# Queries and keys of an attention kernel by seven half products in place of eight

## The chip, the cores and the metric

One core of a Trainium2 chip runs the whole program; the time is device microseconds of that core. The engines that matter are PE (TensorE, matrix products into PSUM), DVE (VectorE), ACT (ScalarE), POOL (GpSimd, which works on SBUF only), and SP, whose queue issues nearly all DMAs. Each engine takes its instructions in order and waits for the others by semaphores. The order on every engine is written out by hand in this kernel.

## The reference, cut to what matters

Two attention layers run one after the other over 4 images of 32x32 tokens with 768 channels, 12 heads of 64. Each layer normalizes by groups of channels, projects to queries, keys and values, adds relative-position terms to the scores, and projects the result back. Everything is float32.

```python
def _L0_conv_ref(x, Wqkv, Wproj, bproj, rel_pos_h, rel_pos_w):
    ...
    qkv = x @ Wqkv
    ...
    q, k, v = (qkv[0], qkv[1], qkv[2])
    ...
    scores = scale * jnp.einsum('bqc,bkc->bqk', q, k) + bias
    attn = jax.nn.softmax(scores, axis=-1)
    out = jnp.einsum('bqk,bkc->bqc', attn, v)
    ...
    return out @ Wproj + bproj
...
x = x + _L0_conv_ref(_gn(x), ...)
x = x + _L1_conv_ref(_gn(x), ...)
```

Layer 1 is of the same form, with biases on queries, keys and values.

## The kernel before

The kernel walks over 8 images (4 for each layer) and, in each, over 6 pairs of heads; `g` counts the 48 pairs. A pair is 8 units, one for each 128 query tokens (`n` = 0 to 7). A unit emits, in this order: the DMAs in the list `early`; `biases` for the unit two ahead (two POOL additions of 128x1024, L323); `scores` for the unit one ahead (PE L337, then on DVE an addition with a minimum, L346, then the exponential on ACT, L350); the reads of turned weights that have come due; up to 3 steps of `take` (in unit 7 alone); `turn` for the present unit (two DVE transposes L370, then a DMA to memory, read back later as `pt`); `divide` for the unit one ahead (reciprocal on DVE L358, then head 0 is scaled on POOL L362 and head 1 on ACT L364); the rest of `take`; and in units 2 and 6 `weigh` (PE L399, the weighted sum of values, copied out by ACT as `attn`).

`take` hands out the steps of the list `todo`: the projections that the next pair needs (`prepare`) and a share of the output projection (`put_out`, in unit 7). `shares` says how many steps each unit takes. A projection of queries or keys, `project_in`, makes 512 tokens of one of the two: 6 chunks of 128 channels, and for each chunk two products of 64 rows, one in the upper half and one in the lower half of the array's rows (L215). The two halves go to two banks of PSUM; ACT copies one out and DVE adds the other (L228/L230, L231). A pair has four such groups, eight half products over the 64-row halves of the channels. `project_values` makes 256 tokens of values for two pairs at once, in the same two row halves (L250, evacuated by L260 on ACT and L261 on DVE, two of each in alternation). `positions` (PE L282, ACT L287 and L297) and `diagonals` (8 small DMAs, L309) make the position terms from 512 tokens of queries.

All PE results but the scores share one ring of two PSUM tiles, `ps_m`: a group of matmuls starts when the group two before it in the order of PE has been evacuated. The scores have a ring of their own, `ps_s`. Six `sc` tiles hold the scores of three units.

Near the end of an image the next one is prepared: its normalization statistics are gathered in pair 3 (`norm`), and in pair 4 `apply` normalizes its six tiles of 128x1024 in place on DVE (L194): one in each of units 2, 4 and 6, and three in unit 7.

Of the kernel before, what the change touches and what calls it, by code (L numbers as in the profile page):

```python
# [36 lines left out]
P = 128  # L37
# [13 lines left out]
AHEAD = 3  # L51
# [3 lines left out]
def attention_blocks(ctx: ExitStack, tc: tile.TileContext, a: dict, out: bass.AP):  # L55
# [4 lines left out]
    wpool = ctx.enter_context(tc.tile_pool(name="weights", bufs=2))  # L60
    wopool = ctx.enter_context(tc.tile_pool(name="wo", bufs=2))
    xpool = ctx.enter_context(tc.tile_pool(name="x", bufs=NC + AHEAD))
    apool = ctx.enter_context(tc.tile_pool(name="attn", bufs=6))
    qkpool = ctx.enter_context(tc.tile_pool(name="qk", bufs=2))
    vpool = ctx.enter_context(tc.tile_pool(name="v", bufs=3))
    scpool = ctx.enter_context(tc.tile_pool(name="sc", bufs=6))
    tmppool = ctx.enter_context(tc.tile_pool(name="tmp", bufs=2))
    tbpool = ctx.enter_context(tc.tile_pool(name="tb", bufs=2))
    ptpool = ctx.enter_context(tc.tile_pool(name="pt", bufs=2))
    relpool = ctx.enter_context(tc.tile_pool(name="rel", bufs=2))  # L70
    iopool = ctx.enter_context(tc.tile_pool(name="io", bufs=4))
# [15 lines left out]
    xn_of, w_of, wo_of = {im: [] for im in range(NI)}, {}, {}  # L87

    def load_x(im, c, chunk=None):

        l, b = images[im]
        if c == len(xn_of[im]):
            xn_of[im].append(xpool.tile([P, S], FP, tag="xn", name=f"xn_{im}_{c}"))
        chunk = c if chunk is None else chunk
        nc.sync.dma_start(out=xn_of[im][c], in_=srcs[l][b][chunk * P : (chunk + 1) * P, :])

    def load_w(g, which):

        im, pair = divmod(g, NP)
        if which == 2:  # L100
            w = wpool.tile([P, NC, 2 * P], FP, tag="wv", bufs=1, name=f"wv_{g}")
            src = a[f"wv{images[im][0]}"][pair // 2]
        else:
            w = wpool.tile([P, NC, P], FP, tag="w", name=f"w_{g}_{which}")
            src = a[f"wqk{images[im][0]}"][pair, which]
        w_of[g, which] = w
        nc.sync.dma_start(out=w, in_=src.rearrange("p (c o) -> p c o", c=NC))

    for c in range(NC):
        load_x(0, c)  # L110
    for which in range(3):
        load_w(0, which)
# [35 lines left out]
    def stats(im, c, i, x):  # L148

        if i == 0:  # L150
            half_stats[im] = small.tile([P, 2, 6], FP, tag="st", name=f"st_{im}_{c}")
        st = half_stats[im]
        nc.vector.bn_stats(st[:, i, :], x)  # L153
        if i == 1:
            nc.vector.bn_aggr(mv_of[im][:, c, :], st.rearrange("p i s -> p (i s)"))

    def norm(im):
# [13 lines left out]
        def gather():  # L171
            queue.dma_start(out=per.rearrange("(c p) s -> p c s", p=P), in_=mv_of[im])
# [11 lines left out]
        def inverses():  # L184
            nc.vector.reciprocal(mv[:, 2, 0:1], mv[:, 2, 1:2])
            for k, x in enumerate((mv[:, 0, 0:1], mv[:, 2, 0:1])):
                nc.vector.tensor_copy(g[:, 1, :, k], x.to_broadcast([NG, GS]))
            queue.dma_start(out=back.rearrange("(g k) s -> g k s", k=GS), in_=g[:, 1, :, :])

        def spread():  # L190
            queue.dma_start(out=nrm, in_=back.rearrange("(c p) s -> p c s", p=P))

        def apply(c):
            nc.vector.tensor_scalar(  # L194
                xn_of[im][c], xn_of[im][c], nrm[:, c, 0:1], nrm[:, c, 1:2], ALU.subtract, ALU.mult
            )

        return {1: gather, 2: by_group, 4: groups, 5: inverses, 7: spread}, apply


    qk_of, v_of, rel_of, t_of = {}, {}, {}, {}

    def project_in(g, which, i):

        im, pair = divmod(g, NP)
        xn, w = xn_of[im], w_of[g, which]
        cols = slice(i * HALF, (i + 1) * HALF)
        if i == 0:
            tag = "qk"[which]
            qk_of[g, which] = qkpool.tile([P, S], FP, tag=tag, name=f"{tag}_{g}")  # L210
        t = ps_m.tile([P, 2, HALF], FP, tag="m", name=f"pj_{g}_{which}_{i}")
        for c in range(NC):
            for a in range(2):
                rows = slice(a * D, (a + 1) * D)
                nc.tensor.matmul(  # L215
                    t[:, a, :], lhsT=w[rows, c, :], rhs=xn[c][rows, cols],
                    start=(c == 0), stop=(c == NC - 1),
                )
            if c < NC - 1:
                yield True  # L220
        to, t = qk_of[g, which], [t[:, a, :] for a in range(2)]
        if which == 1:
            to = to.rearrange("p (a m) -> p a m", a=4)[:, :, i * P : (i + 1) * P]
            t = [x.rearrange("p (m a) -> p a m", a=4) for x in t]
        else:
            to = to[:, cols]
        if images[im][0] == 0:
            nc.scalar.copy(to, t[0])  # L228
        else:
            nc.scalar.activation(to, t[0], AF.Identity, bias=bqkv[:, which, pair : pair + 1])  # L230
        nc.vector.tensor_tensor(to, t[1], to, ALU.add)  # L231
        if which == 0:
            (later if g else mid).append(lambda: positions(g, i))
        if i == 1 and g + 1 < NPAIR:
            later.append(lambda: load_w(g + 1, which))
        yield True

    def project_values(g, i):

        im, pair = divmod(g, NP)  # L240
        xn, w = xn_of[im], w_of[g, 2]
# [4 lines left out]
        for k in range(2):  # L246
            for c in range(NC):
                for a in range(2):
# [3 lines left out]
                        lhsT=xn[c][rows, (2 * i + k) * P : (2 * i + k + 1) * P], rhs=w[rows, c, :],  # L252
# [9 lines left out]
        if i == 3:  # L262
            if g + 2 < NPAIR:
# [422 lines left out]
```

## Time and profile before

| | before |
|---|---|
| median of 3 runs | 3512.72 us (3509.97 to 3515.46) |
| the profiled execution | 3513.09 us, of which the span is 3511.3 us |
| granted TensorE clock | 0.998 |
| busy: DVE, ACT, POOL | 2306.5, 1810.3, 2290.3 us |
| DMA | 1046.75 MB, mean 298 GB/s |
| steady period of one pair (start of an output projection to the next, 317.60 to 389.29) | 71.69 us |
| the same where an image ends (389.29 to 462.05) | 72.76 us |

A busy share is the time in which an engine has an instruction in work. The chain of waits is the work that ended last, followed back from the end of the program; a stretch that is wholly on PE in it is one in which PE waited for nothing. In the timeline each line has the start, the length, the engine, the line of the kernel, the operation, what it writes and reads, and in brackets how long the engine was idle before it and what it waited for. Lengths of successive DVE instructions overlap a little: an addition of 692 ns on 512 elements is followed by the next instruction 0.61 us after its start, a pair of transposes takes 2.28 us, and two L346 take 2.29 us.

### The profile page before, as it was taken

The numbers are of one execution on the slowest core, as the hardware profiler recorded it, in microseconds if no ns is written. First come the engines' busy times: TensorE is split into PE (matmuls) and PEld (weight loads), VectorE is DVE, ScalarE is ACT, GpSimd is POOL, SyncE is SP. The second block draws the span as 40 slices with busy tenths as digits, with TensorE's granted clock in tenths as the row PEclk, the third lists the DMA queues.
The fourth block names the chain that finished last, engine by engine and source line by source line (L and its number), as shares of the span: only waits on it lengthen the run. The fifth ranks groups of instructions, "written<-read, shape, count | busy, mean of one in ns | idle before, by whom it ended". The sixth has DMA issues, their size and how long they took to land.

```text
span 3511.3 us, 55069 instructions
## 1 busy us (share of the span) xinstructions
PE 3460.9 (99%) x21120; PEld 1920.0 (55%) x21120; DVE 2306.5 (66%) x3532; ACT 1810.3 (52%) x2913; POOL 2290.3 (65%) x1154
## 2 busy tenths in 40 slices
PE   6999999999999999999999999999999999999998
PEld 3555555555555555555555555555555555555553
DVE  4766767767677676666766667666666666666665
ACT  3555545554545545455545555455545555455543
POOL 3776666666666666666666666666666666666662
PEclk9999999999999999999999999999999999999999
DMA  3988988889898888988888988888888888888877
GB/s 129 321 299 290 322 306 308 316 285 316 301 321 308 295 313 290 320 303 285 310 306 314 305 287 309 311 305 300 297 305 316 307 292 301 310 297 291 293 275 264
DMA packets 520407, 1046.75 MB, mean 298 GB/s; under 512 B 142672, under 2 KB 205648, under 8 KB 470992
## 3 DMA queue, kind: packets, MB, share of 16 engines
q1 hardware_dynamic: 465648, 1015.81, 82.9%
q10 hardware_dynamic: 54496, 27.43, 2.6%
q8 instruction: 166, 2.72, 0.3%
q14 instruction: 97, 0.79, 0.1%
HBM read 568.01 MB, written 475.10 MB: 297 GB/s over the span
## 4 chain that ended last, share of the span: by engine, by line
PE 94%; DVE 2%; DMA 2%; issue 1%; ACT 0%; SPq 0%; DVEq 0%; ACTq 0%
PE pj L215 26%; PE av L399 19%; PE s L337 19%; PE pv L250 14%; PE o L471 14%; PE tp L282 2%; DMA td<-tb 1%; DVE tb L370 1%; DVE sc L346 1%; DMA pt<-td 0%; DVE st L153 0%; DVE q L231 0%; DVE res L482 0%; DMA per<-mv 0%; ACT q L230 0%
## 5 line engine op out<-in xcount | busy, mean ns | idle before, releaser
L323 POOL TENSOR_TENSOR sc<-rel 128x1024 f32<-128x1024 f32 x768 | 1881.2, 2473 | 48.3 <-DMA rel<-tdr 33.6
L350 ACT ACTIVATE sc<-sc,sm 128x1024 f32<-128x1024 f32 x768 | 880.3, 1147 | 792.1 <-DVE sm L346 790.6
L346 DVE CUSTOM_DVE_ANT_0 sc<-s,sc 128x1024 f32<-128x1024 f32 x768 | 908.2, 1220 | 438.3 <-issue 221.5
L362 POOL TENSOR_SCALAR sc<-sc,sm 128x1024 f32<-128x1024 f32 x376 | 420.3, 1118 | 1099.5 <-DVE sm L358 1069.0
L215 PE MATMUL pj<-xn,w 64*128 64x512 f32 x4608 | 1032.5, 591 | 26.9 <-DVE xn L194 25.9
L370 DVE STREAM_TRANSPOSE tb<-sc 128x1024 f32<-128x1024 f32 x768 | 907.9, 1220 | 14.6 <-DMA td<-tb 12.9
L215 PEld LDWEIGHTS pj<-xn,w 64*128 64x128 f32 x4608 | 452.2, 188 | 569.3 <-issue 527.6
L337 PE MATMUL s<-k,q 64*128 64x512 f32 x3072 | 751.1, 598 | 6.6 <-DVE sm L346 6.4
L364 ACT ACTIVATE sc<-sc,sm 128x1024 f32<-128x1024 f32 x392 | 449.2, 1148 | 499.6 <-DVE sm L358 499.6
L399 PE MATMUL av<-pt,v 128*64 128x256 f32 x6144 | 684.7, 381 | 10.1 <-DVE q L231 7.7
L399 PEld LDWEIGHTS av<-pt,v 128*64 128x64 f32 x6144 | 432.9, 137 | 291.6 <-DVE q L231 41.6
L250 PE MATMUL pv<-wv,xn 64*128 64x256 f32 x4608 | 515.7, 376 | 0.0
L250 PEld LDWEIGHTS pv<-wv,xn 64*128 64x128 f32 x4608 | 448.7, 187 | 90.5 <-issue 33.4
L471 PE MATMUL o<-attn,wo 128*128 128x512 f32 x1080 | 476.3, 597 | 0.0
L337 PEld LDWEIGHTS s<-k,q 64*128 64x128 f32 x3072 | 288.7, 187 | 299.9 <-issue 268.8
L471 PEld LDWEIGHTS o<-attn,wo 128*128 128x128 f32 x1080 | 201.5, 190 | 271.4 <-issue 254.9
L261 DVE TENSOR_TENSOR v<-pv,v 128x256 f32<-128x256 f32 x192 | 81.5, 425 | 240.1 <-ACT v L260 240.1
L231 DVE TENSOR_TENSOR k<-pj,k 128x512 f32<-128x512 f32 x96 | 66.4, 692 | 182.3 <-ACT k L228 93.1
L231 DVE TENSOR_TENSOR q<-pj,q 128x512 f32<-128x512 f32 x96 | 66.4, 692 | 171.8 <-ACT q L230 85.9
L260 ACT COPY v<-pv 128x256 f32<-128x256 f32 x192 | 70.5, 367 | 189.8 <-PE pv L250 142.7
L297 ACT COPY rel<-tp 32x256 f32<-32x256 f32 x384 | 139.4, 363 | 53.9 <-ACT t L287 27.8
L350 ACT ACTIVATION_READ_ACCUMULATOR sc<-sc,sm 128x1 f32 x768 | 143.2, 187 | 0.0
(36 smaller groups left out, 941.7 us busy)
## 6 DMA issues: line engine op xcount, KB each, us to landing
td<-tb SPq DMA_DIRECT2D x384, 1024.0 KB, 5.7
pt<-td SPq DMA_DIRECT2D x382, 1024.0 KB, 8.8
w<-in_wqk SPq DMA_DIRECT2D x96, 384.0 KB, 5.7
tdr<-t ACTq DMA_DIRECT2D x96, 256.0 KB, 8.0
part<-res SPq DMA_DIRECT2D x84, 256.0 KB, 4.7
res<-part SPq DMA_DIRECT2D x84, 256.0 KB, 7.5
wv<-in_wv SPq DMA_DIRECT2D x24, 768.0 KB, 6.6
wo<-in_wo SPq DMA_DIRECT2D x90, 192.0 KB, 7.1
```

The lines of the kernel that those rows point to most:

```text
L215: nc.tensor.matmul(t[:, a, :], lhsT=w[rows, c, :], rhs=xn[c][rows, cols], start=(c == 0), stop=(c == NC - 1),)
L250: nc.tensor.matmul(t[:, a, k, :], lhsT=xn[c][rows, (2 * i + k) * P : (2 * i + k + 1) * P], rhs=w[rows, c, :], start=(c == 0), stop=(c == N ...
L297: nc.scalar.copy(rel_of[g][rows, :, 0, 4 * i : 4 * i + 4, :], src)
L323: nc.gpsimd.tensor_tensor(sc.rearrange("p (a k) (u l) -> p a (k u) l", a=4, l=8), rel[:, h, 0, n, :].unsqueeze(1).unsqueeze(3).to_broadcas ...
L337: nc.tensor.matmul(ps[h][:, cols], lhsT=q[rows, n * P : (n + 1) * P], rhs=k[rows, cols], start=True, stop=True,)
L346: nc.vector.tensor_tensor_reduce(out=sc, in0=ps[h], in1=sc, scale=-scale, scalar=BIG, op0=ALU.add, op1=ALU.min, accum_out=st[:, 0, h : h + 1],
L350: nc.scalar.activation(sc, sc, AF.Exp, bias=st[:, 0, h : h + 1], scale=-1.0, accum_out=st[:, 1, h : h + 1],)
L362: nc.gpsimd.tensor_scalar(sc, sc, st[:, 2, h : h + 1], 1.0, ALU.mult, ALU.mult)
L364: nc.scalar.mul(sc, sc, st[:, 2, h : h + 1])
L370: nc.vector.transpose(tb[:, :, h, :], sc_of[g, n, h])
L399: nc.tensor.matmul(av[rows, at * 2 * P : (at + 1) * 2 * P], lhsT=v_of[g][:, k, rows], rhs=pt_of[g, quarter].rearrange("p n r k h i -> p (n ...
L471: nc.tensor.matmul(t, lhsT=wo_of[im, o, c], rhs=attn_of[im * NP + c][:, cols], start=(c == c0), stop=(c == c1 - 1),)
```

## The change

The four groups of a pair become four kinds of `products` with seven half products. With the 64-channel halves of a chunk called L and H, the two halves of the tokens 0 and 1, and the weights qL, qH, kL, kH:

| kind | upper row half | lower row half | steps |
|---|---|---|---|
| 0 | qL x0L | qH x0H | 6 |
| 1 | b s | kH (x0H - s) | 6 |
| 2 | (kH - kL)(x0L - x1L), chunks 0 to 2 | the same, chunks 3 to 5 | 3 |
| 3 | (kL - qL)(x1L + x1H) | (qH - b) x1H | 6 |

with b = kH - kL + qL and s = x1L + x1H - x0L. Sums of these give the queries and keys of all 1024 tokens: eight DVE additions (L231 before had four) and one ACT copy (four before).

The weights have to be combined for each pair (`combine`, in units 1 to 3 of the pair before: two DVE subtractions of 64x768 in unit 1, a half-width DVE and a half-width POOL subtraction and an ACT copy in unit 2, a POOL subtraction of 64x768 in unit 3), the activations once for each image (`sums`: 15 DVE and 9 POOL operations of 64x512 and 12 ACT copies, laid over units 5 of pair 4 to 3 of pair 5), and the value weights once for two pairs (`combine_values`, in units 4, 5 and 7 of odd pairs: an ACT copy and a DVE subtraction of 64x512 each), since x1L is overwritten by x1L + x1H.

Around it: the channels are laid out in another order by the host, so that the halves L and H of the six chunks are the first and the second 384 channels; x is held in 128x512 tiles, 18 of them (before: 9 of 128x1024); `apply` runs on ACT for most tiles, twice in each of units 1 to 6 of pair 4; the weights of queries and keys have one buffer each instead of two; the `tmp` tile that `positions` and `combine_values` share has one buffer instead of two; the values come second in `todo`, so that `project_values` runs in units 1 and 3; the second `positions` moves to unit 7; `diagonals` is called twice for a pair, with 8 DMAs of half the size each; the scatter and gather of `norm` take two DMAs each; and `stats` is emitted in place rather than one unit later.

```diff
-    wpool = ctx.enter_context(tc.tile_pool(name="weights", bufs=2))
+    wpool = ctx.enter_context(tc.tile_pool(name="weights", bufs=1))
...
-    vpool = ctx.enter_context(tc.tile_pool(name="v", bufs=3))
+    vpool = ctx.enter_context(tc.tile_pool(name="v", bufs=4))
...
-    tmppool = ctx.enter_context(tc.tile_pool(name="tmp", bufs=2))
+    tmppool = ctx.enter_context(tc.tile_pool(name="tmp", bufs=1))
...
+    def combine(g, stage):
+
+        wa, wb, wc, wd = (weights_of(g, name) for name in "abcd")
+        first, second = slice(0, NC // 2), slice(NC // 2, NC)
+        if stage == 0:
+            nc.vector.tensor_tensor(wc[LO], wc[LO], wa[LO], ALU.subtract)
+            nc.vector.tensor_tensor(wb[LO], wb[LO], wc[LO], ALU.subtract)
+        elif stage == 1:
+            nc.scalar.copy(wb[HI], wb[LO])
+            nc.gpsimd.tensor_tensor(wd[LO], wb[LO, first], wa[LO, first], ALU.subtract)
+            nc.vector.tensor_tensor(wd[HI], wb[LO, second], wa[LO, second], ALU.subtract)
+        else:
+            nc.gpsimd.tensor_tensor(wb[HI], wa[HI], wb[HI], ALU.subtract)
+
+    def combine_values(g, j):
+
+        w = wv_of[g]
+        part = slice(2 * j, 2 * j + 2)
+        t = tmppool.tile([P, 2, 2 * P], FP, tag="tmp", name=f"tv_{g}_{j}")
+        nc.scalar.copy(t[HI], w[LO, part])
+        nc.vector.tensor_tensor(w[HI, part], w[HI, part], t[HI], ALU.subtract)
...
+        def apply(c, h, scalar=True):
+            x = xn_of[im][h][c]
+            if scalar:
+                nc.scalar.activation(x, x, AF.Identity, bias=nrm[:, c, 1:2], scale=nrm[:, c, 0:1])
+            else:
+                nc.vector.tensor_scalar(
+                    x, x, nrm[:, c, 0:1], nrm[:, c, 1:2], ALU.mult, ALU.add
+                )
...
+    def sums(im, c, stage):
+
+        x0, x1 = xn_of[im][0][c], xn_of[im][1][c]
+        if stage == 0:
+            s24_of[im, c] = spool.tile([P, HALF], FP, tag="s24", name=f"s24_{im}_{c}")
+            if c < NC // 2:
+                s3_of[im, c] = spool.tile([P, HALF], FP, tag="s3", bufs=NC // 2, name=f"s3_{im}_{c}")
+                nc.gpsimd.tensor_tensor(s3_of[im, c][LO], x0[LO], x1[LO], ALU.subtract)
+            nc.scalar.copy(s24_of[im, c][LO], x1[HI])
+        s24 = s24_of[im, c]
+        if stage == 1:
+            if c >= NC // 2:
+                nc.vector.tensor_tensor(s3_of[im, c - NC // 2][HI], x0[LO], x1[LO], ALU.subtract)
+            nc.vector.tensor_tensor(x1[LO], x1[LO], s24[LO], ALU.add)
+            nc.vector.tensor_tensor(s24[LO], x1[LO], x0[LO], ALU.subtract)
+        elif stage == 2:
+            nc.scalar.copy(s24[HI], s24[LO])
+        elif stage == 3:
+            nc.gpsimd.tensor_tensor(s24[HI], x0[HI], s24[HI], ALU.subtract)
...
+        if kind == 0:
+            nc.scalar.copy(qs[1], ts[0])
+            add(qs[0], ts[1], qs[1], 0)
+            (later if g else mid).append(lambda: positions(g, 0))
+        elif kind == 1:
+            add(ks[1], turned(ts[0]), turned(qs[1]))
+            add(ks[0], turned(ts[1]), ks[1], 1)
+        elif kind == 2:
+            add(ks[1], turned(ts[0]), ks[1])
+            add(ks[1], turned(ts[1]), ks[1])
         else:
...
+            add(whole(qs[1]), whole(ts[1]), back(ks[1]), 0)
+            add(ks[0], turned(ts[0]), ks[0])
+            add(ks[1], turned(ts[0]), ks[1], 1)
+            (later if g else mid).append(lambda: positions(g, 1))
+            if g + 1 < NPAIR:
+                later.append(lambda: (load_w(g + 1, "c"), load_w(g + 1, "b")))
...
-        if i == 1:
-            later.append(lambda: diagonals(g))
+        later.append(lambda: diagonals(g, i))
...
+        counts = [NC, NC, NC // 2, NC]
+        groups = [(products(g, kind), counts[kind]) for kind in range(4)]
+        return groups[:1] + values + groups[1:]
...
+    applies = {1: (0, (0, 1)), 2: (0, (2, 3)), 3: (0, (4, 5)), 4: (1, (0, 1)), 5: (1, (2, 3)), 6: (1, (4, 5))}
+    sum_steps = {
+        (4, 5): [(0, (0, 1))],
+        (4, 6): [(1, (0, 1)), (0, (2, 3))],
+        (4, 7): [(2, (0, 1)), (1, (2,)), (1, (3,)), (0, (4, 5))],
+        (5, 0): [(3, (0, 1)), (2, (2,)), (1, (4,))],
+        (5, 1): [(3, (2,)), (2, (3, 4))],
+        (5, 2): [(3, (3, 4)), (1, (5,))],
+        (5, 3): [(2, (5,)), (3, (5,))],
+    }
...
-                shares = [6, 6, 0, 6, 12, 6, 0, 12]
+                shares = [6, 6, 0, 6, 9, 6, 0, 12]
...
+            if n == 3 and 0 < g + 1 < NPAIR - 1:
+                later.append(lambda: load_w(g + 2, "a"))
...
             turn(g, n)
             if at + 1 < len(units):
                 divide(*units[at + 1])
-            if pair == 4 and n == 7 and not end:
...
+            if n in (1, 2, 3) and g + 1 < NPAIR:
+                combine(g + 1, n - 1)
+            if n in (4, 5, 7) and pair % 2 and g + 1 < NPAIR:
+                combine_values(g + 1, (4, 5, 7).index(n))
+            if pair == 4 and n in applies and not end:
+                for c in applies[n][1]:
+                    apply(c, applies[n][0])
+            if not end:
+                for stage, chunks in sum_steps.get((pair, n), ()):
                     for c in chunks:
-                        apply(c)
+                        sums(im + 1, c, stage)
             take(todo, share)
```

In this list the new calls stand behind `divide` and ahead of the rest of `take`, so on each engine they come after the reciprocal or the scaling of the unit and before the evacuation of the groups that `take` hands out there.

## The prediction

> **What bounds the kernel.** I read the page's busy times and its chain first, then the waits of PE, then the timeline of one pair in the middle, engine by engine.
>
> ```profile
> PE 3460.9 (99%) x21120; PEld 1920.0 (55%) x21120; DVE 2306.5 (66%) x3532; ACT 1810.3 (52%) x2913; POOL 2290.3 (65%) x1154
> ...
> PE 94%; DVE 2%; DMA 2%; issue 1%; ACT 0%; SPq 0%; DVEq 0%; ACTq 0%
> PE pj L215 26%; PE av L399 19%; PE s L337 19%; PE pv L250 14%; PE o L471 14%; PE tp L282 2%; DMA td<-tb 1%; DVE tb L370 1%; DVE sc L346 1%; DMA pt<-td 0%; DVE st L153 0%; DVE q L231 0%; DVE res L482 0%; DMA per<-mv 0%; ACT q L230 0%
> ```
>
> The chain lies 94% on PE, so PE's time saved is time saved, as long as nothing else becomes late. The timeline of PE from unit 1 to unit 2 of a pair shows how near the next thing is:
>
> ```profile
> 1628.71 1.88 PE L337 MATMUL s<-k,q 64*128 64x512 f32 x8
> 1630.43 5.32 PE L215 MATMUL pj<-xn,w 64*128 64x512 f32 x24
> 1635.58 1.06 PE L282 MATMUL tp<-tab,q 64*128 64x128 f32 x16
> 1636.47 1.89 PE L337 MATMUL s<-k,q 64*128 64x512 f32 x8
> 1638.29 7.13 PE L399 MATMUL av<-pt,v 128*64 128x256 f32 x64
> ```
>
> and on DVE in the same stretch:
>
> ```profile
> 1635.43 0.12 DVE L358 RECIPROCAL sm<-sm 128x2 f32<-128x2 f32 x1
> 1637.24 0.69 DVE L231 TENSOR_TENSOR q<-pj,q 128x512 f32<-128x512 f32 x1 [1.69 <-ACT q L228]
> ```
>
> The weighing (L399) needs the PSUM tile that this addition frees at 1637.93. It starts at 1638.29: 0.36 us of slack. The third view is the old `apply` on DVE and what POOL does beside it, first with POOL idle (six of them), then one by one in unit 7 of pair 4:
>
> ```profile
> 24.98 4.42 DVE L194 TENSOR_SCALAR xn<-xn,nrm 128x1024 f32<-128x1024 f32 x6 [3.46 <-DMA nrm<-back]
> 1689.46 1.20 DVE L194 TENSOR_SCALAR xn<-xn,nrm 128x1024 f32<-128x1024 f32 x1
> 1690.58 2.90 DVE L194 TENSOR_SCALAR xn<-xn,nrm 128x1024 f32<-128x1024 f32 x1
> 1694.07 2.26 DVE L194 TENSOR_SCALAR xn<-xn,nrm 128x1024 f32<-128x1024 f32 x1
> ```
>
> ```profile
> 1690.08 2.86 POOL L323 TENSOR_TENSOR sc<-rel 128x1024 f32<-128x1024 f32 x1
> 1692.89 2.88 POOL L323 TENSOR_TENSOR sc<-rel 128x1024 f32<-128x1024 f32 x1
> ```
>
> Alone an apply takes 4.42 / 6 = 0.74 us; beside POOL 1.20 to 2.90. The second one, begun at 1690.58, ends at 1693.48, some 0.55 us after POOL's addition ended (1692.94); and POOL's additions, 2.46 us in the median, take 0.4 longer there. So the two engines take turns, whole instruction by whole instruction, and the one that waits comes next.
>
> **PE's gain.** A step of `project_in` (two products of 64x512) is 5.15 / 6 = 0.86 us (1630.43 to 1635.58). A pair goes from 24 to 21 steps: 3 x 0.86 = 2.57 us, 48 pairs: -123 us. With nothing else late a pair would take 71.69 - 2.57 = 69.1.
>
> **The new DVE operations.** The additions of `products` read one operand in PSUM, as L231, L346 and L484 do, which never stretch beside POOL: 0.61 us each. The subtractions of `combine`, `combine_values` and `sums` read two operands in SBUF; no DVE row of before does that. Lower bound: no waiting, 0.61 us at 512 elements, 0.88 at 768 (0.61 plus half of 1.14 - 0.61, one transpose of 1024 being 1.14). Upper bound: they take turns with POOL as L194 does. I take the upper end: L194 is the nearest row, the only large one with its data in SBUF alone.
>
> [...]
>
> **Where this delays PE.** Each place by both ends, with time counted from a unit's first PE instruction.
>
> *Unit 1 to 2, every pair.* The weighing could start at 9.58, as before. The reciprocal is over at 6.75, then two dependent subtractions: free, to 8.5. Taking turns: 6.75 to 7.63, POOL's scaling (asked at 6.94) 7.63 to 8.73, second 8.73 to 9.61. Then the values are evacuated: DVE, ACT, DVE, 1.3 us by L261's rows. Free 9.8, taking turns 11.0: stalls of 0.25 and 1.4 us.
>
> *Units 4 to 6, odd pairs.* `combine_values` stands ahead of the evacuations. Its ACT copy is ready 1.85 us after the reciprocal (0.16, scaling 1.06, copy 0.57); POOL has scaled by then (0.2 + 1.1) and begun the first of two additions of 2.45, so the subtraction waits for that and DVE is free 4.4 us after the reciprocal (free case: 2.5). In unit 4 L346 starts at 2.6, behind the values' evacuation, and two of them (2.29) and the transposes (2.28) put the reciprocal's end at 7.15. DVE is free at 11.55 and frees kind 1's tile with two additions at 12.8; kind 3 could have started at 9.45 + 1.72 = 11.2: 1.6 us (free: none). DVE goes on with kind 2's additions to 14.0, unit 5's softmax (4.6 to the reciprocal) to 18.6, 4.4 to 23.0, kind 3's three additions to 24.85, unit 6's reciprocal at 29.45; behind it ACT scales (1.2) and copies `attn` (0.6), 31.3, which frees the tile of the first output group. PE: kind 3 from 12.8 to 17.95, scores 1.8 and weighing 7.06 to 26.8, `positions` 1.0, scores 1.9, ready at 29.7: 1.6 more (free: none).
>
> *Unit 7, odd pairs.* The first group's evacuation, transposes and reciprocal are over 5.9 us after that group starts, `combine_values` at 10.3, the second group's evacuation at 10.9; the fourth group needs its tile at 7.8: 3.1 us. Free, the copy still waits for `tmp`, which `positions` has just given to a DMA (tdr lands after 8.0): some 2.1.
>
> *Unit 7 of pair 4 (7 images).* Five subtractions ahead of the second group's evacuation, and POOL's scaling and two additions in turn: 5 x 0.61 + 1.1 + 2 x 2.45 = 9.05 us. The four of unit 6 have already made DVE 4 us late. Stalls 1.8 + 9.4 = 11.2 (free: 1.8).
>
> *Units 0 to 4 of pair 5 (7 images).* Three subtractions in unit 0, three in unit 2, five POOL operations (1.3 us each, 2.46 x 512 / 1024 plus start) before unit 3 ends: the weighing 3.3 us later than in other pairs, kind 1's last chunk 0.9: 4.2 (free: 1).
>
> **What lies beside other work.** `apply` on ACT: 12 x 0.67 us an image (L230) behind ACT's scaling, ahead only of the values' copies; DVE loses 84 us of L194, which removes the 1.07 us stall of each of 7 images (72.76 - 71.69 in the table of before): -7.5. If ACT ran late, the exponentials would hold the reciprocals. POOL's `combine` (1.0 and 1.9 us a pair) fits in its waits for the reciprocal, 1069 us in 365 of 384 units; without that cover up to 2.9 us a pair. DMAs: 192 KB more a pair, 9.4 MB on 1047; eight more issues of 0.51 us on SP (4.09 us for eight), now in unit 0 ahead of the reads of `pt`. Those land at about 1624 + 8.8 = 1632.8 for a weighing at 1638.3: 1 to 4 us late still fits, past 5.5 each us costs one. `load_w` "a" waits on SP in unit 4 for POOL's subtraction, 2.9 us, ahead of reads that have 18 us. The second `positions` moves as it is. The strided additions of kinds 1 and 3 may cost 0.61 to 1.2 each, 1.2 a pair at most and mostly in DVE's idle time. The prologue does two value groups instead of one ahead of the first scores and has them less after: 0, with 5 us either way.
>
> **Sum.** -123 + 48 x 1.4 (67) + 23 odd pairs x 6.3 (145; 1.6 + 1.6 + 3.1) + 7 x 11.2 (78) + 7 x 4.2 (29) - 7.5 = +189. On the span of 3511.3 that is 3700; what lies around the span (1.8 us, 3513.09) and the median (3512.72, 0.4 below) don't matter to this. **Forecast: 3700 us**, own range 3600 to 3790 (half of the stalls at the three last places off, or a queue behind them).
>
> **Rivals.** *No turns taken*: DVE's subtractions run at 0.61 and 0.88 whatever POOL does. -123 + 48 x 0.25 (12) + 23 x 2.1 (48) + 7 x 1.8 (13) + 7 x 1 (7) - 7.5 = -50: 3461, faster. For it: L346 and L261, also two-operand instructions, never stretch. Against: they have one operand in PSUM. It decides below some 0.7 us of waiting for a subtraction; the forecast has 1.1 to 2.4 at most places. *Nothing waits*: -123 - 7.5, 3381; against it stands unit 7 of odd pairs, where `tmp`'s single buffer holds the copy with no port at all. *Half a turn*: a subtraction is slowed but not held for a whole addition, about half of the way between: 3580, slower.
>
> **Chances.** Forecast 0.70, half a turn 0.12, no turns 0.15, nothing waits 0.03. A measurement tells 0.2% (7 us) from no change. Faster by more: the last two cases, less 0.01 for stalls that I underrate, 0.17; within 0.2%: 0.03, that 0.01 and 0.02 of half a turn; slower: 0.80. The range leaves out about 0.1 below (half of no turns and nothing waits) and 0.1 above: 3460 to 3790.
>
> **What would show it.** Right: the subtractions of `combine` with a mean well over 0.96 us and their longest over 2; PE idle before L399 in unit 2, in odd pairs before kind 3 and the fourth output group of unit 7, ended by DVE; an odd pair near 77 us, an even one near 71, pairs 4 and 5 near 81. Wrong: subtractions at 0.7 and 0.96 us, and pairs of 69 to 72 us: then the first rival. Wrong too, if PE waits mostly for `pt` (SP's queue) or for ACT behind its applies, which I cost at nothing.

## The result, and the profile after

The changed kernel takes **3851.39 us** (median of 4 runs, 3848.64 to 3859.78) against 3513.66 us for the kernel before beside it (4 runs): 1.0967 times as long, 95% interval 1.0947 to 1.0986. The forecast was 3700 us: slower, as forecast, but +337 us where the sum had +189. The time lies outside the range.

The page of the changed kernel, its busy times, its chain and its clock:

```profile
PE 3458.7 (90%) x20544; PEld 1957.6 (51%) x20544; DVE 2890.1 (75%) x4026; ACT 1926.7 (50%) x3075; POOL 2647.7 (69%) x1322
...
PEclk9999999999999999999999998999989999999999
...
PE 57%; DVE 22%; issue 7%; DMA 7%; ACT 5%; POOL 2%; SPq 0%; DVEq 0%; ACTq 0%; POOLq 0%
```

The chain has left PE: 94% before, 57% now, and 22% on DVE. The first line holds a riddle: PE has 576 matmul instructions fewer (each product is two in the trace) and is busy as long as before (3460.9). The clock line hardly helps, since a slice of 96 us hides a stretch of a few; the mean granted clock is 0.966 (0.998 before).

The waits of PE (what waits, what it waits for, us in all, times, longest):

```profile
PE o L572 <- DVE res L583: 105.1, 27, 8.6
PE av L500 <- issue: 80.8, 45, 4.1
PE pj L303 <- DVE xn L249: 29.2, 1, 29.2
PE o L572 <- ACT attn L511: 28.6, 16, 3.0
PE pj L303 <- DVE k L320: 27.7, 12, 2.9
PE pj L303 <- DVE k L318: 25.4, 12, 3.3
PE o L572 <- DVE res L585: 22.5, 7, 3.5
PE o L572 <- ACT attn L509: 20.8, 14, 2.0
PE s L438 <- DVE sm L447: 17.9, 9, 5.8
PE pj L303 <- DVE v L367: 13.3, 1, 13.3
PE av L500 <- DMA pt<-td: 6.2, 3, 4.2
```

Most end at an evacuation on DVE. Another 49.4 us, nearly all in unit 7, end at ACT's copy of `attn` ahead of the first output group. The weighing's 80.8 us are put down to "issue": they are 45 places, all in unit 2, where it starts about 0.1 us after the values' addition on DVE (L367) that frees its PSUM tile. The DMA that brings `pt` accounts for 6.2 us, so SP's queue is not the matter. The first 29.2 us were there before (25.9).

DVE's groups (busy us, mean ns of one, then the idle time before them):

```profile
L150 DVE TENSOR_TENSOR wv<-wv,tv 64x512 f32<-64x512 f32 x72 | 153.3, 2129 | 133.2 <-ACT tv L149 133.2
L318 DVE TENSOR_TENSOR k<-pj,k 128x512 f32<-128x512 f32 x192 | 130.1, 688 | 15.0 <-PE pj L303 8.9
L270 DVE TENSOR_TENSOR xn<-xn,s 64x512 f32<-64x512 f32 x48 | 102.4, 2134 | 4.5 <-ACT s L265 2.3 <-POOL s L264 1.2
L136 DVE TENSOR_TENSOR wb<-wb,wc 64x768 f32<-64x768 f32 x48 | 83.4, 1738 | 1.7
...
L318 DVE TENSOR_TENSOR k<-pj,q 128x512 f32<-128x512 f32 x48 | 51.8, 1080 | 0.8
```

An addition with one operand in PSUM takes 0.69 us as before (L318, `k<-pj,k`); with both in SBUF three times as long (L270, half the partitions and the same elements). The last line is a strided one: 1.08.

How long one can wait is shown by unit 6 to 7 of a pair 4. DVE:

```profile
2321.04 0.66 DVE L270 TENSOR_TENSOR xn<-xn,s 64x512 f32<-64x512 f32 x1
2321.74 1.49 DVE L271 TENSOR_TENSOR s<-xn,xn 64x512 f32<-64x512 f32 x1
2323.15 6.47 DVE L270 TENSOR_TENSOR xn<-xn,s 64x512 f32<-64x512 f32 x1
2329.65 0.68 DVE L271 TENSOR_TENSOR s<-xn,xn 64x512 f32<-64x512 f32 x1
```

and POOL beside it:

```profile
2321.22 1.47 POOL L463 TENSOR_SCALAR sc<-sc,sm 128x1024 f32<-128x1024 f32 x1 [2.23 <-DVE sm L459]
2322.66 1.69 POOL L264 TENSOR_TENSOR s<-xn,xn 64x512 f32<-64x512 f32 x1
2324.31 4.76 POOL L424 TENSOR_TENSOR sc<-rel 128x1024 f32<-128x1024 f32 x2
```

An addition of one kind and size takes 0.66 us and then 6.47: the long one ends 0.55 us after the last of three POOL instructions in a row (at 2329.07). The same holds throughout. Of the two-input instructions of `sums` and `combine_values`, 131 last over 1.3 us, and all end 0.53 to 0.56 us after a POOL instruction did; the 54 long ones of 64x768 in `combine` end 0.80 to 0.82 us after one. So a waiting instruction ends as if it had begun when POOL's ended: what comes behind that is some 0.1 us less than its length without a wait (0.66 to 0.69 us for 64x512, 0.92 to 0.95 for 64x768). In 178 of these 185 it waited for one POOL instruction, in 7 (one for each image that is prepared) for three.

What such delays cost PE is seen a unit later: the output group that waits for DVE, and then PE and its clock in the stretch behind (busy us and number of PE, PEld, DVE, ACT, POOL; granted clock, DMA share, GB/s).

```profile
2344.75 4.86 PE L572 MATMUL o<-attn,wo 128*128 128x512 f32 x6 [8.09 <-DVE res L583]
```

```profile
core 0: us, PE busy (x) PEld busy (x) DVE busy (x) ACT busy (x) POOL busy (x), PEclk, DMA share, GB/s
2342.00:2348.80 6.80, 4.05 (x5) 1.85 (x6) 3.32 (x4) 0.00 (x0) 0.77 (x1) 0.50 0.28 108
2351.00:2361.00 10.00, 10.00 (x62) 5.74 (x60) 9.23 (x12) 4.74 (x7) 4.44 (x3) 1.00 0.96 342
```

PE is idle for 8.09 us, and the six matmul instructions behind that take 0.81 us each, where they follow each other in 0.43 otherwise: the clock is granted at one half. This is what the forecast left out. The clock records have 50 such stretches of 1.6 to 13.7 us, 261.0 us in all (before: 4, 12.9 us). PE is busy in 203.7 of these (10.2); at half speed, as by the 0.81 us for 0.43, half of that is lost: **101.9 us** (5.1), an estimate. Less this, its work is 3356.8 us, against 3455.8 before: the riddle's answer. (For these sums and those below, PE is idle where no product is in work for over 0.25 us.)

### The profile page after: what moved, and what is told of

The parts are those of the page before. It is cut to its first block, busy times and chain, and to the rows that moved or that the text cites. A ratio compares the mean times of both kernels' runs of the same rounds, so it can differ in the third digit from the quotient of the medians.

```text
span 3846.8 us, 55787 instructions
## 1 busy us (share of the span) xinstructions
PE 3458.7 (90%) x20544; PEld 1957.6 (51%) x20544; DVE 2890.1 (75%) x4026; ACT 1926.7 (50%) x3075; POOL 2647.7 (69%) x1322
## 4 chain that ended last, share of the span: by engine, by line
PE 57%; DVE 22%; issue 7%; DMA 7%; ACT 5%; POOL 2%; SPq 0%; DVEq 0%; ACTq 0%; POOLq 0%
PE pj L303 13%; PE av L500 13%; PE s L438 12%; PE o L572 9%; PE pv L355 8%; DVE tb L471 7%; DVE sc L447 4%; DMA td<-tb 3%; DVE wv L150 2%; DVE xn L270 2%; ACT sc L465 2%; PE tp L384 2%; DVE k L318 1%; DMA tdr<-t 1%; POOL sc L424 1%
## 5 line engine op out<-in xcount | busy, mean ns | idle before, releaser
L463 POOL TENSOR_SCALAR sc<-sc,sm 128x1024 f32<-128x1024 f32 x376 | 478.9, 1274 | 1070.1 <-DVE sm L459 1064.0
L447 DVE CUSTOM_DVE_ANT_0 sc<-s,sc 128x1024 f32<-128x1024 f32 x768 | 907.1, 1218 | 281.1 <-PE s L438 264.9
L500 PE MATMUL av<-pt,v 128*64 128x256 f32 x6144 | 705.6, 389 | 87.9 <-issue 80.8
L438 PE MATMUL s<-k,q 64*128 64x512 f32 x3072 | 759.4, 601 | 18.0 <-DVE sm L447 17.9
L572 PE MATMUL o<-attn,wo 128*128 128x512 f32 x1080 | 540.2, 656 | 178.9 <-DVE res L583 105.1
L303 PE MATMUL pj<-xn,wc 64*128 64x512 f32 x576 | 268.9, 616 | 53.1 <-DVE k L320 27.7
L303 PE MATMUL pj<-xn,wa 64*128 64x512 f32 x1152 | 261.3, 595 | 29.2 <-DVE xn L249 29.2
L303 PE MATMUL pj<-xn,wb 64*128 64x512 f32 x576 | 269.5, 617 | 0.0
L303 PE MATMUL pj<-s,wb 64*128 64x512 f32 x576 | 257.5, 594 | 13.3 <-DVE v L367 13.3
L303 PE MATMUL pj<-s,wc 64*128 64x512 f32 x576 | 257.5, 595 | 0.0
L150 DVE TENSOR_TENSOR wv<-wv,tv 64x512 f32<-64x512 f32 x72 | 153.3, 2129 | 133.2 <-ACT tv L149 133.2
L303 PEld LDWEIGHTS pj<-xn,wc 64*128 64x128 f32 x576 | 110.6, 196 | 195.2 <-issue 192.4
L303 PEld LDWEIGHTS pj<-xn,wa 64*128 64x128 f32 x1152 | 113.9, 189 | 166.1 <-issue 136.1
```

What stands on the lines that cost most here:

```text
L150: nc.vector.tensor_tensor(w[HI, part], w[HI, part], t[HI], ALU.subtract)
L303: nc.tensor.matmul(t[:, h, :], lhsT=w[rows, c, :], rhs=x[c][rows, :], start=(c == 0), stop=(c == n - 1),)
L438: nc.tensor.matmul(ps[h][:, cols], lhsT=q[rows, n * P : (n + 1) * P], rhs=k[rows, cols], start=True, stop=True,)
L447: nc.vector.tensor_tensor_reduce(out=sc, in0=ps[h], in1=sc, scale=-scale, scalar=BIG, op0=ALU.add, op1=ALU.min, accum_out=st[:, 0, h : h + 1],
L463: nc.gpsimd.tensor_scalar(sc, sc, st[:, 2, h : h + 1], 1.0, ALU.mult, ALU.mult)
L500: nc.tensor.matmul(av[rows, at * 2 * P : (at + 1) * 2 * P], lhsT=v_of[g][:, k, rows], rhs=pt_of[g, quarter].rearrange("p n r k h i -> p (n ...
```

## The experiments

One execution of each, with the kernel before at 3513 to 3516 us beside it; the four of the changed kernel lie within 11 us, so a difference of that size between two rows shows nothing. First the sums that they are read by: time, PE's idle time behind the prologue (up to the first reduction) and in it, loss by half clock as above, and the period by the place of a pair in its image (from the first reduction of a pair to the next, mean over images 1 to 6; unit 7's output groups fall to the next pair here).

| kernel | us | idle | prologue | clock | pairs 0, 1, 2, 3 | 4 and 5 |
|---|---|---|---|---|---|---|
| before | 3513 | 18 | 28 | 5 | 71.7 each | 144.6 |
| changed | 3849 | 337 | 47 | 102 | 77.5, 74.9, 76.5, 74.5 | 169.9 |
| calls behind (e1) | 3694 | 176 | 46 | 60 | 70.5, 70.2, 71.2, 71.0 | 168.6 |
| one input (e2) | 3613 | 175 | 40 | 32 | 72.4, 71.3, 73.6, 71.8 | 153.9 |
| filled (e3) | 3810 | 124 | 47 | 40 | 74.8, 73.7, 77.3, 74.1 | 167.9 |
| no strides (e4) | 3837 | 329 | 46 | 102 | 76.6, 73.5, 77.5, 73.3 | 170.7 |
| once a layer (e5) | 3904 | 386 | 47 | 106 | 81.8, 70.7, 83.2, 70.4 | 175.8 |
| the same, behind (e6) | 3947 | 431 | 47 | 87 | 83.5, 71.3, 86.5, 70.0 | 175.7 |
| weights on POOL (e7) | 3656 | 177 | 47 | 60 | 69.6, 71.2, 71.2, 69.8 | 167.5 |
| the same, behind (e8) | 3649 | 162 | 47 | 56 | 69.6, 70.7, 71.6, 69.6 | 166.6 |
| values first (e9) | 3864 | 332 | 43 | 122 | 77.7, 74.9, 76.7, 74.5 | 170.4 |
| sums on POOL (e10) | 3590 | 122 | 47 | 43 | 69.7, 71.2, 71.3, 69.8 | 157.9 |
| sums, one input (e11) | 3566 | 106 | 40 | 42 | 70.2, 70.5, 71.7, 69.8 | 155.0 |

### Turns, and the place of the calls

**e1**: the new calls behind the rest of a unit's matmuls.

```diff
-            if n in (1, 2, 3) and g + 1 < NPAIR:
-                combine(g + 1, n - 1)
...
             take(todo, share)
+            if n in (1, 2, 3) and g + 1 < NPAIR:
+                combine(g + 1, n - 1)
...
             if n == 6:
                 weigh(g, (0, 1))
```

> The changed kernel with the new calls (combine, combine_values, apply, sums) emitted behind the rest of take, so that on DVE the evacuations of the unit's groups come ahead of the subtractions. Theory (subtractions that take turns with POOL hold back the evacuations behind them, and PE waits for those): the idle time of PE ahead of kind 3, of the output groups and of the weighing goes down from about 330 us to under 120, half clock from 261 us to under 100, time 3500 to 3620. Rival (DVE has too much to do whatever the order): 3750 or more, with the idle time of PE moved to other places.

Between the two: 3693.84 us. `combine`'s subtractions even grew (2.00 and 3.03 us mean, from 1.06 and 1.74), yet pairs 0 to 3 lost most of their stalls: a long instruction on DVE cost PE where an evacuation was queued behind it, and little where none was. Pairs 4 and 5 stayed near where they were (168.6), and some idle time moved, as the rival had it: the wait for the softmax's reduction on DVE went from 17.9 to 59.8 us.

**e2**: each DVE instruction with two inputs in SBUF becomes a transpose of one operand, of the same size, so that the combined weights and the sums of half tiles are not computed.

```diff
-            nc.vector.tensor_tensor(wc[LO], wc[LO], wa[LO], ALU.subtract)
+            nc.vector.transpose(blocks(wc[LO]), blocks(wa[LO]))
```

> Every DVE subtraction and addition of two SBUF operands (combine, combine_values, sums) replaced by a DVE transpose of one of them of the same size; the products then work on other numbers. Theory (two SBUF operands on DVE take turns with POOL): the replacements last 0.7 us at 512 elements and 0.96 at 768 where the subtractions had 2.13 and 1.74, POOL's additions go back from 2.54 to 2.46 us, and the time falls to 3460 to 3540. Rival (it is the number of DVE instructions and their place in the order): 3750 or more, the replacements no shorter in effect.

3613.31 us. Its groups on DVE:

```profile
L156 DVE STREAM_TRANSPOSE wv<-tv 64x512 f32<-64x512 f32 x72 | 51.0, 708 | 134.3 <-ACT tv L155 134.3
...
L142 DVE STREAM_TRANSPOSE wb<-wc 64x768 f32<-64x768 f32 x48 | 46.6, 970 | 1.6
...
L276 DVE STREAM_TRANSPOSE xn<-s 64x512 f32<-64x512 f32 x48 | 33.1, 689 | 3.3 <-ACT s L271 2.3 <-POOL s L270 0.7
```

With one input they take 0.71, 0.97 and 0.69 us for 2.13, 1.74 and 2.13, and POOL's two large groups are back at 2.47 and 1.12 us (changed: 2.54 and 1.27). Taking the turns away takes off 235 us, more than any other single edit here; this overlaps with what e1 takes off (155), so the two don't add up. But some 100 us over the kernel before remain without any such turn. The theory allowed 25 at most, the rival 235 or more, so neither range holds. What stands ahead of the evacuations still is DVE's own 0.7 to 1.0 us each and the wait for ACT's copy (134 us over 72, 1.9 each); that these make up the 100 us is argued, not shown.

**e4**: the two strided additions read their operand in SBUF without a stride (keys and queries then hold values in other places).

> The two additions that read queries and keys with a stride (the first of kind 1 and the first of kind 3) read them without it; their values change places. Theory (the stride costs 0.39 us each, 1.08 against 0.69, and counts only where kind 3 waits for kind 1's tile): 0.69 us each, kind 3's stall in odd pairs shorter by about 0.4 us, time 3820 to 3845. Rival (the strides are a main part of the loss, through DVE's length): under 3780.

3836.91 us, in the theory's range, and the additions take 0.68 and 0.69 us. The strides are worth 12 us at most, which is the spread of the changed kernel itself.

### The clock

**e3**: products that nothing reads are put on PE where it stalls.

> The changed kernel with useless products of 64x512 on PE where it waited: one pair of them ahead of the scores of every unit 2, two in unit 5 of odd pairs 1 and 3, three ahead of the fourth output group of odd pairs, two and seven in unit 7 of pair 4, four in unit 2 of pair 5; about 250 us more work for PE. Theory (after a stall PE's clock is halved for 3 to 10 us, and that is the part of the loss that the sum left out): half clock falls from 261 us to under 80, and the kernel with more work is faster, 3730 to 3800. Rival (the stalls cost their own length alone): the time is the same or longer, 3850 to 3950.

3809.61 us: over 200 us of work added, and 39 us faster. By the table's sums: PE's work at full clock 3357 to 3589, +232; idle 384 to 170, -214; clock -62; together -44. (The time fell by 39; the other 5 are gaps under 0.25 us, which these sums leave out.) The idle time is exchanged for work nearly one for one, and what is left is the clock. The half clock is 92 us in all, not under 80, and the time 10 us over the upper bound given.

**e12**: the kernel *before*, with one pause of PE a pair.

```diff
+            if n == 4 and 0 < im < NI - 1:
+                pause(g, (2, 4, 6, 8, 11, 16)[pair])
             if at + 1 < len(units):
                 scores(*units[at + 1])
```

> The kernel before the change, with one pause of PE a pair in images 1 to 6, in unit 4: a small product, a chain of 2, 4, 6, 8, 11 or 16 copies of 128 elements on ACT (by the pair's number in the image), and a product that reads the last copy; nothing reads that. By the nearest copies (0.36 us for 256 elements) the pauses are about 0.7, 1.2, 1.8, 2.4, 3.3 and 4.8 us long, 14 us an image. Theory (a pause beyond some 2 to 3 us brings a stretch at half clock, in which PE does half as much): pairs with a pause under 2 us grow by its length and 0.3, those with 3 us and more by 1.7 to 3.4 us beyond their length; 3515 plus 86 for the pauses, 10 for the products and 25 to 70 for the clock: 3615 to 3680. Rival (the half clock in the changed kernel comes from something else in it, and a pause costs its length): no half clock behind the pauses, each pair grows by the pause and 0.3, 3590 to 3615.

3728.73 us, 49 over the theory's range: the pauses were longer than estimated, 1.6, 2.3, 2.9, 3.6, 4.6 and 6.2 us, and a pair with a pause takes 1.2 us beyond it even without half clock, not 0.3. Two of them in PE's timeline:

```profile
1047.61 0.49 PE L326 MATMUL pause<-z,q 128*128 128x128 f32 x2 [2.27 <-ACT z L324]
1048.03 2.11 PE L349 MATMUL s<-k,q 64*128 64x512 f32 x8
...
1201.67 0.80 PE L326 MATMUL pause<-z,q 128*128 128x128 f32 x2 [3.59 <-ACT z L324]
1202.39 3.91 PE L349 MATMUL s<-k,q 64*128 64x512 f32 x8
```

and the windows behind them:

```profile
1048.00:1050.50 2.50, 2.50 (x13) 1.90 (x14) 0.34 (x1) 0.00 (x0) 2.50 (x2) 1.00 0.98 394
1202.00:1206.00 4.00, 4.00 (x11) 2.21 (x12) 0.00 (x0) 0.00 (x0) 1.29 (x1) 0.50 0.40 71
```

Behind 2.27 us of idle the scores take 2.11 us, behind 3.59 us 3.91, at a granted clock of 0.50. A stretch at half clock followed 2 of 6 pauses of 1.6 us, none of 2.3, 4 of 6 of 2.9, and all 18 of 3.6 us and more. Where pauses of one length fell out both ways the price is bare: with 2.9 us a pair takes 75.8 to 75.9 us, or 77.5 to 77.6 with a stretch of 3.4 us: 1.7, half of the stretch. Half of PE's busy time in the stretch is 1.6 to 2.7 us for the pauses that brought one (3.3 once, with a stretch of 10.2 us). The rival falls: no other part of the change is in this kernel. The changed kernel agrees: a half stretch began during or within 6 us after 1 of 65 idle times of 0.8 to 2 us, 26 of 51 of 2 to 3 us, and 22 of 23 longer ones.

The length of a pause alone does not decide, and the clock records show what goes with the half clock. All changes of the granted clock in a trace lie on one grid of 3.413 us (in the changed kernel's, 99 changes within 1 ns of it). Cut each trace into the pieces of its grid and take those at full clock, over all 14 traces: all 335 in which no product was in work for more than 2.1 us are followed by a piece at half clock, and only 3 of the 13,629 with less than 1.4 us; in between it is 103 of 399. (In the changed kernel's trace alone: 38 of 38, none of 943, and 11 of 59.) This accounts for how the pauses of one length fell out. One of 2.27 us was cut by an edge into 1.26 and 1.01 us and brought nothing; one of 1.61 us lay in a single piece and brought 3.4 us at half clock.

### Weights and activations

**e5, e6**: weights combined only in the first image of a layer, stored, and read back for the other three.

```diff
+        if im % B and name != "a":
+            nc.sync.dma_start(out=w, in_=kept[images[im][0], pair, name])
...
+        if g // NP % B:
+            if j == 2:
+                later.append(lambda: nc.sync.dma_start(out=w[HI], in_=kept[images[g // NP][0], g % NP, "v"]))
+            return
```

> The weights are combined only in the first image of each layer (12 of 48 pairs), stored in device memory and read back whole for the other three images; the additions on the activations, and the place of every call, stay. Theory (the weights' subtractions on DVE, in turns with POOL, are what holds PE up in pairs 0 to 3, and the pauses bring the half clock): pairs 0 to 3 of the six other images fall from 75 to 77 us to 69 to 70, and pairs 4 and 5 together from 170 to about 150, so 3520 to 3650, with half clock under 130 us. Rival 1 (the activations' additions are the main cost): pairs 4 and 5 keep 165 or more, and the time stays above 3680. Rival 2 (the transfers that are added, about 1.4 MB a pair, make PE wait for weights): PE waits in front of the projections for a DMA on wb, wc, wd or wv, and the time is above 3700.

> As the run before (weights combined once a layer and read back), and the new calls are emitted behind the rest of a unit's matmuls, ahead of the weighing, as in the run with the calls behind. Theory (two separate costs, the turns and the place of the calls in front of the evacuations): it takes off what is left in pairs 4 and 5 by the place, so 3480 to 3580, 40 to 90 us below the run before. Rival (with the weights gone there is room on DVE for the additions and their place does not matter any more): within 20 us of the run before.

Both theories missed, 3903.91 and 3947.41 us, and pairs 4 and 5 kept 175.8 and 175.7, as e5's first rival had it. The page of waits of e5 says where the most was lost:

```profile
PE pv L377 <- DMA wv<-kept_v: 217.0, 18, 16.3
```

The upper half of `wv` can be read back only after the first values are made with the raw one, so it was issued at the end of the odd pair and landed 12.5 us later (median). That is a cost of this edit's own, by the second rival's mechanism; in e6 the same wait is 296.4 us. Where no such load falls, in pairs 1 and 3, the images with weights read back have 69.4 to 70.9 us and next to no idle time.

**e7**: all subtractions of weights on POOL. **e8**: the same with the calls behind.

```diff
-            nc.vector.tensor_tensor(wc[LO], wc[LO], wa[LO], ALU.subtract)
+            nc.gpsimd.tensor_tensor(wc[LO], wc[LO], wa[LO], ALU.subtract)
```

> All subtractions on the weights (five a pair, three more in odd pairs) go to POOL; the calls stay where they are, the activations' additions stay as they are. Theory (DVE's own time and the turns behind POOL hold up the evacuations): without two-input work on the weights DVE is free, pairs 0 to 3 fall to 69 to 72 us, and the time to 3560 to 3700; POOL goes from 2648 to about 2980 us busy. Rival (POOL, already 69% busy, falls behind, its bias additions come late and DVE's reduction waits for sc from POOL): DVE waits for POOL over 150 us, PE for the reduction, above 3800.

> As the run before (the weights' subtractions on POOL), and the new calls behind the rest of a unit's matmuls. Theory: pairs 0 to 3 at 69 to 70.5 us, pairs 4 and 5 at about 160 together as far as the activations' additions go, 3500 to 3620. Rival (POOL in order: its subtractions now stand nearer to the next bias additions, and these come late): slower than the run before.

3655.95 us, as expected; 3648.62, some 29 over its range, since pairs 4 and 5 kept 166.6 us. Pairs 0 to 3 are now near the 69.4 us that a pair takes where PE waits for nothing, *without* the calls being moved: POOL's waits for the reciprocal hold the five subtractions (1.8 us for 64x768), and DVE's queue is clear ahead of the evacuations. So weights on DVE cost pairs 0 to 3; what is left lies in pairs 4 and 5, where the activations' additions stand.

**e10**: on top of e8, the activations' additions of images 1 to 7 on POOL, and POOL's scaling of eight units an image on DVE (the expectation says ten; the edit and the trace have eight). **e11**: on top of e8, these additions replaced by DVE transposes of one operand.

> Weights' subtractions on POOL and calls behind, as before, and the activations' additions of images 1 to 7 also on POOL, so that DVE has no instruction with two inputs in SBUF left in pairs 4 and 5; in return DVE takes POOL's scaling by the sums' inverse in ten units of these pairs. Theory (it is the turns with POOL that hold DVE up in pairs 4 and 5): these two pairs fall from 166.6 us together to 140 to 152, the time to 3460 to 3560. Rival (POOL, 95 to 100% busy in these units, cannot take them): the bias additions come late, DVE's reduction waits for sc from POOL, the pairs stay at 166 or more, 3640 or more.

> Weights' subtractions on POOL and calls behind; the activations' additions on DVE are replaced by transposes of one operand of the same size (the sums of half tiles are not computed). Theory (turns): pairs 4 and 5 fall from 166.6 us together to 143 to 156, the time to 3540 to 3600. Rival (the amount of work on DVE, POOL and ACT in these pairs, not the turns): 160 or more, over 3610.

e10: 3589.93 us, 30 over its range, pairs 4 and 5 at 157.9. It does not take the turns away, since the scaling that DVE took over waits for POOL too. It takes 2.89 us on average, for the 0.74 of `apply`, of the same operation and size, with POOL idle in the kernel before:

```profile
L465 DVE TENSOR_SCALAR sc<-sc,sm 128x1024 f32<-128x1024 f32 x56 | 161.8, 2889 | 2.0
```

e11: 3566.30 us and 155.0, both in range. By e11 the turns of the additions are 12 us of the 28 that these two pairs lose in e8 against 138.8 (2 x 69.4). The other 16 are left over, put down here to the work itself on DVE, ACT and POOL and to the clock behind its stalls; no run separates these. e10, the fastest here in which nothing of the computation is left out, stays 2.2% over the kernel before. e11 leaves the sums out and is 1.5% over it, so more than these turns would have to go for the change to pay.

### The prologue

**e9**: the first two groups of values ahead of the second half's applies and of the additions.

> The changed kernel with one move in its prologue: the first two groups of value products stand ahead of the applies of the second half and of the additions on the activations. Theory (the prologue is 25 us longer because the values' evacuation stands behind eighteen additions on DVE, and PE idles 13.3 us for it): that wait goes, the first scores start at 68 to 78 us instead of 81.6, the time falls by 4 to 13 us to 3838 to 3848. Rival (the chain of applies, additions and copies itself sets the end of the prologue): the first scores stay within 2 us of 81.6, PE waits as long for the sums instead, and the time stays at 3849 to 3855.

Neither: 3864.20 us, and the first reduction came 6 us later (90.1 for 83.8). The 13.3 us for `v` went, but the additions now start behind the values' evacuation, PE waits 7.5 us for one of them, and the clock is lower in that stretch (0.67 from 60 to 84 us, 0.82 in the changed kernel). My theory of this wait falls. That the chain of applies, copies and additions on DVE, ACT and POOL sets the end of the prologue fits this, and fits e2, in which transposes stand in place of the additions and the first reduction comes 6.5 us earlier (77.3); no run isolates it.

## Why the prediction was half right

**The stalls were right in sum, and near by place.** The terms of the sum that are stalls make 67 + 145 + 78 + 29 = 319 us, less the old 7.5. Measured, behind the prologue: 337.1 less the 17.7 that were there before, 319.4 for 311.5. By place:

| place | forecast, us each | measured |
|---|---|---|
| weighing in unit 2 | 1.4 | 1.3 to 1.6 |
| kind 3, pairs 1 and 3 | 1.6 | 2.5 and 2.7 |
| output groups, odd pairs | 1.6 + 3.1 | 3.7, 4.6 and 4.8 |
| unit 7 of pair 4 | 11.2 | 11.3 |
| weighing in unit 2 of pair 5 | 1.4 + 3.3 | 4.1 |
| kind 1's last chunk, pair 5 | 0.9 | none |

Part of this nearness is luck. Kind 3 lost 52 us where the forecast had 37 (23 x 1.6), the output groups of odd pairs 100 for 108, the weighing in pair 5 29 for 39 (7 x 5.6): errors that cancel. And two terms do not follow from their own working: 9.61 + 1.3 is 10.9, a stall of 1.3 and not 1.4, and the 9.4 in "1.8 + 9.4" has no source beside the 9.05 worked out ahead of it.

The mechanism held too: DVE and POOL by turns, which e2 shows by taking the two inputs away. "The one that waits comes next" held for 178 of 185 long instructions; at 2323.15 and six times more DVE waited for three POOL instructions. Of the signs named, the mean of `combine`'s subtractions was 1.06 and 1.74 us, but none lasted over 2 (1.79 the longest); those of `combine_values` and `sums` did, up to 2.9 and 6.5.

**The step that failed is the sum**: "-123 + 48 x 1.4 ..." prices a stall at its own length and PE's work at full clock. It has no term for what a stall does to the clock. That term is 101.9 - 5.1 = **97 us**, two thirds of the 147 us that were missing in the span (3846.8 against 3700). e12 shows it in the kernel before alone, and e3 that filling the stalls gives it back. The profile of before had the hint: its own four stretches at half clock are in the records, and the granted clock was in the table.

**PE's gain was too large**: 3455.8 to 3356.8 is 99 us, not 123. A pair that waits for nothing takes 69.4 us, so 2.3 and not 2.57 were gained, 13 us over 48 pairs; where the other 11 went was not traced.

**The prologue was not "0, with 5 us either way"**: 18.3 us more of idle time (46.6 for 28.3); as far as is known, the reason is in e9. I had counted value groups, and not the 15 additions of `sums` and the three applies on DVE ahead of the first kind 1.

Together: 319.4 + 18.3 + 97 - 99 = +335.7, and the span grew by 335.5 (from 3511.3).

**Costed at nothing, rightly**: the reads of `pt` (6.2 us here, though 19 to 32 us in e7, e8, e10 and e11, where other stalls are gone) and SP's queue. Behind the prologue no wait of PE ends at `apply` on ACT, though no run moved it alone. The strided additions took 1.08 us, inside 0.61 to 1.2; e4 puts the whole at 12 us or less.

**The rivals.** *No turns taken* (3461) was the fair opposite, and e2 made it true: 3613. It allowed 12 + 48 + 13 + 7 = 80 us for the places; e2 lost 175 - 18 = 157 behind the prologue, 12 in it and 27 more by the clock. So without any turns the change would still have been slower. *Nothing waits* (3381) is what a pair of 69.4 us throughout would come near to; e7 and e8 come near it in pairs 0 to 3 only (69.6 to 71.6). *Half a turn* (3580) did not occur: all 185 long instructions ended 0.53 to 0.56 us (512 elements) or 0.80 to 0.82 us (768) after one of POOL's, so they were held and not slowed.

## What to carry to other kernels

Price a stall of PE by its length and by the clock behind it: in e12 a pause that brought the half clock lost another 1.6 to 2.7 us to it (3.3 once), and the changed kernel's 384 us of idle time came with 102 us lost so. Whether short stalls within one piece of 3.413 us add up is not shown: in the changed kernel's trace each of the 97 full-clock pieces with over 1.4 us of idle time has one gap over 0.25 us. When work is moved off the bounding engine, ask of each new instruction what is queued behind it; the same subtractions cost 5 us a pair on DVE ahead of PE's evacuations (75.9 for 70.5 in pairs 0 to 3) that they did not cost on POOL, which was waiting anyway. And write down first what the preparation costs: a pair gained 2.3 us, 14 an image, and pairs 4 and 5, where an image's additions stand, lost 28 even in e8.

## What the hardware showed beyond that

- Of the 185 long DVE instructions with two inputs in SBUF of the changed kernel, 178 got the next turn behind one POOL instruction, and 7 only behind three in a row: up to 6.5 us, for 0.66 without a wait. Of those with one operand in PSUM, 192 additions (L318, `k<-pj,k`) stayed at 0.67 to 0.70 us and all 768 of L447 at 1.20 to 1.23.
- In the changed kernel half clock came in stretches of 3.4 us and its multiples (27 of 3.4, 18 of 6.8, 3 of 10.2 and 1 of 13.7 among 50; one of 1.6 ends with the record). Over the 14 traces it went not with the length of a gap but with the idle time within one piece of the grid of 3.413 us: it followed 335 of 335 pieces with over 2.1 us, and 3 of 13,629 with under 1.4.
- A DVE addition of 128x512 that reads its operand in SBUF with a stride took 1.08 us in the changed kernel, for 0.68 and 0.69 without one in e4.
